# A two-layer transformer block: norms in two pieces, transposes shared out anew and values one step later in layer 0

## The chip, the cores and the metric

The kernel runs on one core of a Trainium2 chip. The core has TensorE (PE: matmuls, and transposes as matmuls with an identity), VectorE (DVE), ScalarE (ACT), GpSimd (POOL), and SyncE (SP), which here does nothing but issue DMAs. The metric is device time in microseconds (us), from one launch; lower is better. All data is 32-bit float.

## The reference, cut to what matters

The input x is 4 sequences of 256 tokens with 512 features. Two post-norm layers follow each other:

```python
x = _layernorm(x + _L0_attn_ref(x, Wq, bq, Wk, bk, Wv, bv, Wo, bo))   # 32 heads of 16, 8 key heads
x = _layernorm(x + _L0_ffn_ref(x, q_scales, q_vals, bias))            # one 512x512 matmul
x = _layernorm(x + _L1_attn_ref(x, w_qkv, w_o))                       # 32 heads of 128, 8 key heads
x = _layernorm(x + _L1_ffn_ref(x, kernel))                            # one 512x512 matmul
...
scores = jnp.where(causal, scores, NEG)
p = jax.nn.softmax(scores, axis=-1)
out = jnp.einsum('bhqk,bhkd->bhqd', p, v)
```

`_layernorm` subtracts the mean of a row and divides by the square root of its variance plus 1e-5. Only layer 0 matters for most of this document: causal attention over 256 keys, four query heads to a key head, then a projection, a norm, a matmul and a second norm.

## The kernel before, in words

**Steps of layer 0.** The 1,024 tokens are eight tiles of 128. Attention goes through 64 steps (b, qt, h, i): sequence b (4), query tile qt in it (2), half h of the key heads (2), and one of four query heads i that share a key head. A step handles four key heads at once, so 128 queries times 4 heads. With the causal mask, qt = 0 sees one key tile of 128 and qt = 1 sees two, so steps of qt = 1 are about twice as much softmax.

**A step in three parts.** `begin0` (L453) makes the scores on TensorE (L462) into a PSUM tile `sc`, of which there are two (`ps_s0`). VectorE adds the causal mask to the diagonal tile (L467) and takes the row maximum (L470). ScalarE makes four exponentials with their sums (L270). VectorE inverts the sums (L275), and GpSimd divides (L276), which gives `pr`. `transpose0` (L483) turns `pr` so that keys lie on partitions, in `prT`. `end0` (L501) does nothing until the fourth i, and then multiplies the four heads' `prT` with the values (L512) into `o`. After the second half h, `o` is copied to `oT` and a tail is started.

**Two ways to transpose.** `transposed_probabilities` (L286) does it on TensorE, four transposes of 128x128 for a key tile (L291), and ScalarE copies them out of PSUM (L480). `transposed_by_blocks` (L294) has VectorE transpose blocks of 32x32 (L300) into `blocks`; four DMAs write these to a DRAM tile `way` (L306), and one DMA reads them back in order into `prT` (L310). All five are issued by SP. The list `BY_BLOCKS` (L477) chooses: for qt = 0 the steps i = 0 and 2 go through DRAM, for qt = 1 the steps i = 0 and 1, with both their key tiles. The very first query tile, (b, qt) = (0, 0), is done on TensorE altogether.

**The pipeline.** `run` (L315) takes a step per iteration: it begins step n, calls `fill`, transposes step n - `lag`, and ends step n - `lag` - `more`. Layer 0 has `lag=3` and `more=2` (L550), so values come two steps behind the transposes. `fill` (L537) advances two kinds of generators by one piece each: tails, and the projection of the next sequence (`project0`, L352, with pauses from the list `ROOM`), whose GpSimd memset of the value tile `v` (L357) has to wait until the values of two sequences before are used.

**Tails.** `tail0` (L418) does the rest of the layer for one tile of 128 tokens, in pieces: the output projection (L422), the sum with x (L424) and the first norm; two pieces of nothing (one for the last tile); the transposes of x1 (L266); the feed-forward matmul (L437), its sum (L441) and the second norm; two pieces of nothing again; the transposes into `x2T`. `layer_norm` (L252) is five instructions: two of statistics (L256, L257), one of adding epsilon (L258), all on VectorE; the power -1/2 on GpSimd (L259); and on VectorE the subtraction and scaling of the whole tile (L260). The last of these waits for GpSimd.

**Order.** Every engine works through its instructions in the order that they were given. That order is made when the kernel is built, from the program's order, by a scheduler with estimated costs; it moves an instruction ahead of others that it expects to wait. Only few are held to the program's order (`keep_in_program_order`). Semaphores then make each wait for its data and for its buffers: two `prT`, six `pr`, two `blocks` tiles of two key tiles each, four `way`, three PSUM banks for all else (`ps_w`).

**Layer 1** follows with matmuls in a scheme that needs seven products for eight, and softmax steps that use `transposed_by_blocks` for all but the last key head.

Of the kernel before, what the change touches and what calls it, by code (L numbers as in the profile page):

```python
# [12 lines left out]
F32 = mybir.dt.float32  # L13
# [3 lines left out]
ALU = mybir.AluOpType  # L17
# [3 lines left out]
P = 128  # L21
B, S, D = 4, 256, 512
NTT = B * S // P
NC = D // P
NKV, G = 8, 4
# [34 lines left out]
def block_kernel(  # L60
# [62 lines left out]
    a0 = pool(la, "a0", 2, side="right")  # L123
# [7 lines left out]
    def bank_t(name):  # L131
        return ring[0].tile([P, 4, P], F32, tag=ring[1], name=name)

    def bank_m(name):
        return ps_w.tile([P, D], F32, tag="w", name=name)
# [113 lines left out]
        )  # L249


    def layer_norm(dst, y, name):  # L252
        st = s0.tile([P, 6], F32, tag="bn", name=f"bn_{name}", bufs=4)
        mv = s0.tile([P, 2], F32, tag="mv", name=f"mv_{name}", bufs=4)
        rs = s0.tile([P, 1], F32, tag="rs", name=f"rs_{name}", bufs=4)
        nc.vector.bn_stats(st, y)  # L256
        nc.vector.bn_aggr(mv, st)  # L257
        nc.vector.tensor_scalar(rs, mv[:, 1:2], EPS, 1.0, ALU.add, ALU.mult)  # L258
        powers.append(nc.gpsimd.tensor_tensor(rs, rs, minus_half, ALU.pow))  # L259
        nc.vector.tensor_scalar(dst, y, mv[:, 0:1], rs, ALU.subtract, ALU.mult)  # L260

    def transposed(dst, src, name):

        pt = bank_t(f"pt_{name}")
        for c in range(NC):
            nc.tensor.transpose(pt[:, c, :], src[:, ts(c, P)], ident)  # L266
        evacuate(dst, pt)
# [17 lines left out]

    def transposed_probabilities(name, pr, parts, copy=evacuate):  # L286

        for kt, dst in enumerate(parts):
            pt = bank_t(f"pt_{name}_{kt}")
            for i in range(G):  # L290
                nc.tensor.transpose(pt[:, i, :], pr[:, i, ts(kt, P)], ident)  # L291
            copy(dst, pt)

    def transposed_by_blocks(sp, name, pr, nt, dst, bufs):  # L294

        blocks = sp.tile([P, 2, 4, G, 32], F32, tag="blocks", name=f"blocks_{name}", bufs=bufs)
        for kt in range(nt):
            nc.vector.transpose(  # L300
                blocks[:, kt].rearrange("p j h q -> p h j q"),
                pr[:, :, ts(kt, P)].rearrange("p h (j k) -> p h j k", k=32),
            )
        way = dram.tile([2, 4, 32, 4, G * 32], F32, tag="way", name=f"way_{name}")
        for i in range(4):
            nc.sync.dma_start(  # L306
                way[0:nt, :, :, i, :].rearrange("t j k f -> k (t j) f"),
                blocks[32 * i : 32 * i + 32, 0:nt].rearrange("k t j h q -> k (t j) (h q)"),
            )
# [106 lines left out]
    x2 = {}  # L416

    def tail0(tt, oT):  # L418

        py = bank_m(f"py_{tt}")  # L420
        for i in range(G):
            nc.tensor.matmul(py, oT[:, i, :], wop[:, i, :], start=(i == 0), stop=(i == G - 1))  # L422
        y = s0.tile([P, D], F32, tag="y", name=f"y_{tt}")
        nc.vector.tensor_tensor(y, py, x[tt], ALU.add)  # L424
        x1 = s0.tile([P, D], F32, tag="x1", name=f"x1_{tt}")
        layer_norm(x1, y, f"a{tt}")
        yield True
        yield True
        if tt < NTT - 1:
            yield True  # L430
        x1T = s0.tile([P, NC, P], F32, tag="x1T", name=f"x1T_{tt}")
        transposed(x1T, x1, f"x1_{tt}")
        nc.gpsimd.tensor_tensor(x1, x1, fb_b, ALU.add)
        yield True
        pf = bank_m(f"pf_{tt}")
        for c in range(NC):
            nc.tensor.matmul(  # L437
                pf, x1T[:, c, :], wfT[:, c, :], start=(c == 0), stop=(c == NC - 1)
            )
        y2 = s0.tile([P, D], F32, tag="y", name=f"y2_{tt}")  # L440
        nc.vector.tensor_tensor(y2, pf, x1, ALU.add)  # L441
        x2[tt] = xp.tile([P, D], F32, tag="x", name=f"x2_{tt}")
        layer_norm(x2[tt], y2, f"b{tt}")
        yield True
        yield True
        if tt < NTT - 1:
            yield True
        transposed(x2T[:, :, ts(tt, P)], x2[tt], f"x2_{tt}")
        yield True
# [24 lines left out]
        return pr  # L474

    open0 = {}
    BY_BLOCKS = [(0, 2), (0, 1)]  # L477

    def ordered_copy(dst, src):
        nc.scalar.copy(dst, src.rearrange("p n (j q) -> p n j q", q=32))  # L480


    def transpose0(b, qt, h, i, pr):  # L483

        name = f"0_{b}_{qt}_{h}_{i}"
        nt = qt + 1
        if i == 0:
            open0["p", h] = a0.tile(
                [P, 2, G, 4, 4, 32], F32, tag="prT", name=f"prT0_{b}_{qt}_{h}"
            )  # L490
        prT = open0["p", h]
        if (b, qt) > (0, 0) and i in BY_BLOCKS[qt]:
            transposed_by_blocks(a0, name, pr, nt, prT[:, 0:nt, i], 2)
        else:
            copy = evacuate if (b, qt) == (0, 0) else ordered_copy
            transposed_probabilities(
                name, pr, [prT[:, kt, i].rearrange("p j n q -> p n j q") for kt in range(nt)], copy
            )
        return prT

    def end0(b, qt, h, i, prT):  # L501
# [35 lines left out]
    def fill():  # L537
# [10 lines left out]
        before0,  # L548
        fill,
        lag=3,  # L550
        more=2,
    )
    la.close()

# [176 lines left out]
    s1 = pool(ctx, "s1", 2)  # L731
# [136 lines left out]
    def merge():  # L868

        b = merges.pop(0)  # L870
        M1, M5, U, M7 = kept[b][:, 0, 0], kept[b][:, 0, 1], kept[b][:, 1, 0], kept[b][:, 1, 1]
        top, low = x2[2 * b], x2[2 * b + 1]
        add = lambda d, s: nc.gpsimd.tensor_tensor(d, d, s, ALU.add)
        add(top[:, 0:HALF], M1)
        add(U, M1)
        add(top[:, HALF:], M5)
        add(top[:, HALF:], U)
        add(U, M7)
        add(low[:, 0:HALF], U)
        add(low[:, HALF:], M5)  # L880
        add(low[:, HALF:], U)
# [61 lines left out]
    def transpose1(kv, b, qt, pr):  # L943
        name = f"1_{kv}_{b}_{qt}"
        nt = qt + 1
        if kv == NKV - 1:
            prT = s1.tile([P, 2, 4, G, 32], F32, tag="prT", name=f"prT_{name}")
            transposed_probabilities(
                name, pr, [prT[:, kt].rearrange("p j h q -> p (j h q)") for kt in range(nt)]
            )  # L950
            return prT
        prT = s1.tile([P, 2, 4, G, 32], F32, tag="prT", name=f"prT_{name}")
        transposed_by_blocks(s1, name, pr, nt, prT[:, 0:nt], 1)
        return prT

    def end1(kv, b, qt, prT):
        o = ps_o.tile([P, G * P], F32, tag="o", name=f"o1_{kv}_{b}_{qt}")
        for kt in range(qt + 1):
            nc.tensor.matmul(  # L959
                o,  # L960
                v1[:, 2 * b + kt, ts(kv, P)],
                prT[:, kt].rearrange("p j h q -> p h j q")
                if kv < NKV - 1
                else prT[:, kt].rearrange("p j h q -> p (j h q)"),
                start=(kt == 0),
                stop=(kt == qt),
            )
        if kv == NKV - 1:
            if merges:
                merge()  # L970
            oT = open1["oT"][:, (2 * b + qt) % NC, :].rearrange("p (i q) -> p i q", q=P)
            evacuate(oT.rearrange("p i q -> p (i q)"), o)
            outputs.append(output1(kv, 2 * b + qt, oT))
            return
        if qt == 0:
            open1["o"] = s1.tile([P, 2, G, P], F32, tag="o2", name=f"o2_{kv}_{b}")
        o2 = open1["o"]
        evacuate(o2[:, qt].rearrange("p i q -> p (i q)"), o)
        if qt == 1:
            outputs.append(outputs1(kv, b, o2))  # L980
# [79 lines left out]
```

## Time and profile before

| what | value |
|---|---|
| median of 3 runs | 989.89 us (987.88 to 992.61) |
| the profiled execution: time, span | 987.82 us, 985.9 us |
| granted TensorE clock, mean | 0.980 |
| TensorE busy | 935.1 us (95%) |
| VectorE busy | 620.6 us (63%) |
| ScalarE busy | 327.3 us (33%) |
| GpSimd busy | 442.8 us (45%) |
| DMA, mean | 99 GB/s |
| layer 0, start to the first product of layer 1 | 294.9 us |
| layer 1 | 691.0 us |

The span is from the first to the last instruction; the time of an execution has some 1.9 us around it. Times of matmuls overlap, and their ends are modelled. A line of waits names the waiting engine and line, what ended the wait, the total in us, the number of waits and the longest. "Issue" stands where the profile shows no releaser, which includes DMAs that landed. In a timeline a line has start, duration, engine, line of the kernel, operation, output and inputs, shapes, count, and in brackets the idle time before it and what ended it.

### The profile page before, as it was taken

Reading aid. Unit: us, or ns where it says so; the run is one execution under the profiler, and the core shown is the slowest. Engines: PE = TensorE matmul, PEld = TensorE weight load, DVE = VectorE, ACT = ScalarE, POOL = GpSimd, SP = SyncE. Lnnn points to the kernel's source line nnn. Section 1 sums busy time; section 2 is a strip of 40 time slices with the busy share of each in tenths; the row PEclk is TensorE's granted clock in tenths of the full one; section 3 lists DMA queues with packets and bytes.
Section 4 is the critical chain, followed back from the end, with each engine's and each line's share of the span. In section 5 each row is a group of like instructions: output and inputs, shape, how many; then the busy total and the mean of one; then the engine's idle time right before and its main releaser. Section 6 shows DMA issues by size and latency. Waiting matters only on the chain.

```text
span 985.9 us, 11321 instructions
## 1 busy us (share of the span) xinstructions
PE 935.1 (95%) x3417; PEld 541.9 (55%) x3417; DVE 620.6 (63%) x1291; ACT 327.3 (33%) x1218; POOL 442.8 (45%) x461
## 2 busy tenths in 40 slices
PE   7999889988889999999999999999999999999996
PEld 5645435443334444566666666566666566657652
DVE  3786756766733445855666676566666566666566
ACT  2556454565522001423222222222222222223442
POOL 2364452553426512444543633634534553457732
PEclk9999979998899999999999999999999999999998
DMA  9444343443332010444433444333453434343001
GB/s 264 151 104 114 79 112 74 97 117 76 71 100 85 22 43 4 104 136 120 140 108 95 125 132 110 122 82 114 116 141 86 108 88 135 78 126 88 0 22 64
DMA packets 106817, 97.50 MB, mean 99 GB/s; under 512 B 8197, under 2 KB 77446, under 8 KB 106758
## 3 DMA queue, kind: packets, MB, share of 16 engines
q1 hardware_dynamic: 105942, 95.36, 35.9%
q10 hardware_dynamic: 816, 1.44, 0.5%
q8 instruction: 27, 0.44, 0.2%
q14 instruction: 32, 0.26, 0.1%
HBM read 61.11 MB, written 35.65 MB: 98 GB/s over the span
## 4 chain that ended last, share of the span: by engine, by line
PE 74%; POOL 8%; DVE 8%; ACT 5%; issue 2%; DMA 1%; SPq 0%; POOLq 0%; DVEq 0%; ACTq 0%
PE p_q L610 18%; PE po L851 14%; PE o L959 7%; PE sc L919 7%; PE p_v L610 5%; PE p_k L610 5%; POOL pr L276 4%; ACT pr L270 4%; PE o L512 3%; PE py L815 3%; PE sc L462 3%; DVE blocks L300 2%; PE pq L383 2%; DVE nm L470 2%; PE py L422 2%
## 5 line engine op out<-in xcount | busy, mean ns | idle before, releaser
L270 ACT ACTIVATE pr<-sc,nm 128x256 f32<-128x256 f32 (+1 forms) x512 | 209.0, 419 | 375.4 <-DVE nm L935 272.1
L276 POOL TENSOR_TENSOR pr<-pr,sums 128x512 f32<-128x512 f32 (+1 forms) x128 | 187.8, 1469 | 275.9 <-DVE sums L275 262.4
L300 DVE STREAM_TRANSPOSE blocks<-pr 128x512 f32<-128x512 f32 x128 | 87.5, 698 | 69.1 <-POOL pr L276 69.1
L927 DVE SCALAR_TENSOR_TENSOR sc<-table,sc 128x128 f32<-128x128 f32 (+1 forms) x256 | 86.2, 356 | 34.1 <-PE sc L919 32.1
L270 ACT ACTIVATION_READ_ACCUMULATOR pr<-sc,nm 128x1 f32 x512 | 103.6, 202 | 0.0
L919 PEld LDWEIGHTS sc<-kT,qT 128*128 128x128 f32 x512 | 82.1, 191 | 35.2 <-issue 28.7
L919 PE MATMUL sc<-kT,qT 128*128 128x256 f32 (+1 forms) x512 | 95.4, 327 | 0.0
L959 PE MATMUL o<-prT,v 128*128 128x512 f32 x192 | 92.9, 592 | 0.0
L625 DVE TENSOR_TENSOR qT<-p_q,qT 128x512 f32<-128x512 f32 x96 | 64.4, 685 | 34.1 <-PE p_q L610 33.4
L462 PE MATMUL sc<-kT,qT 32*128 32x256 f32 (+1 forms) x256 | 64.3, 564 | 11.8 <-ACT pr L270 11.6
L935 DVE TENSOR_REDUCE nm<-sc 128x2 f32<-128x512 f32 (+1 forms) x128 | 70.2, 551 | 1.7
L851 PE MATMUL po<-wo,o 128*128 128x256 f32 x224 | 58.0, 381 | 4.0 <-ACT qT L618 4.0
L470 DVE TENSOR_REDUCE nm<-sc 128x4 f32<-128x512 f32 (+1 forms) x64 | 60.6, 948 | 0.7
L610 PE MATMUL p_q<-x2T,ws_q 128*128 128x512 f32 x128 | 60.0, 592 | 0.0
L102 ACT COPY o<-o 128x512 f32<-128x512 f32 x29 | 17.0, 585 | 128.8 <-PE o L959 128.8
L610 PE MATMUL p_q<-xt,ws_q 128*128 128x512 f32 x128 | 57.8, 593 | 1.8 <-POOL ws_q L593 1.8
L467 DVE TENSOR_TENSOR sc<-sc,causal 128x512 f32<-128x512 f32 x64 | 43.9, 687 | 22.9 <-PE sc L462 22.6
L610 PE MATMUL p_q<-x2T,wq 128*128 128x512 f32 x128 | 57.6, 592 | 0.0
L851 PE MATMUL po<-wo,so 128*128 128x256 f32 x224 | 57.5, 379 | 0.0
L512 PE MATMUL o<-prT,v 128*32 128x512 f32 x192 | 53.0, 654 | 2.0 <-issue 2.0
L851 PE MATMUL po<-to,so 128*128 128x256 f32 x224 | 52.9, 379 | 0.0
L851 PEld LDWEIGHTS po<-to,so 128*128 128x128 f32 x224 | 42.6, 190 | 16.9 <-issue 12.2
(160 smaller groups left out, 1406.2 us busy)
## 6 DMA issues: line engine op xcount, KB each, us to landing
way<-blocks SPq DMA_DIRECT2D x176, 128.0 KB, 2.5
prT<-way SPq DMA_DIRECT2D x44, 512.0 KB, 3.7
way<-blocks SPq DMA_DIRECT2D x160, 64.0 KB, 1.8
prT<-way SPq DMA_DIRECT2D x40, 256.0 KB, 2.7
wq<-in_L_attn_w_qkv_dram SPq DMA_DIRECT2D x8, 1024.0 KB, 5.2
wo<-in_L_attn_w_o_dram SPq DMA_DIRECT2D x8, 1024.0 KB, 5.9
wk<-in_L_attn_w_qkv_dram SPq DMA_DIRECT2D x4, 512.0 KB, 4.4
wv<-in_L_attn_w_qkv_dram SPq DMA_DIRECT2D x2, 1024.0 KB, 5.1
```

Source lines behind the costliest of these rows:

```text
L270: nc.scalar.activation(pr[:, i, 0:w], sc, AF.Exp, bias=nm[:, i : i + 1], accum_out=sums[:, i : i + 1])
L276: nc.gpsimd.tensor_tensor(pr[:, :, 0:w], pr[:, :, 0:w], sums.unsqueeze(2).to_broadcast([P, G, w]), ALU.mult)
L300: nc.vector.transpose(blocks[:, kt].rearrange("p j h q -> p h j q"), pr[:, :, ts(kt, P)].rearrange("p h (j k) -> p h j k", k=32),)
L462: nc.tensor.matmul(sc[:, j, :, 0:w], qT[rows, i, ts(qt, P)], kT[rows, :, 0:w], start=True, stop=True)
L470: nc.vector.tensor_reduce(nm, scf[:, :, 0:w], AX.X, ALU.max, negate=True)
L512: nc.tensor.matmul(o[32 * r : 32 * r + 32, :], v[:, kt, r, ts(e, 32)], prT[:, kt, :, :, 2 * j + e, :], start=(kt == 0 and e == 0), stop=(k ...
L610: nc.tensor.matmul(bank, fixed, moving, start=(c == 0), stop=(c == 1))
L851: nc.tensor.matmul(bank[:, ts(n, HALF)], left[:, c, :], right[:, c, :], start=(c == 0), stop=(c == 1),)
L919: nc.tensor.matmul(sc[:, m, 0:w], qT[:, 2 * j + m, b * S + qt * P : b * S + (qt + 1) * P], kT[:, b * S : b * S + w], start=True, stop=True,)
L927: nc.vector.scalar_tensor_tensor(sc[:, m, 0:w], table[:, 2 * P - w :], slopes[kv * G + 2 * j + m], sc[:, m, 0:w], ALU.mult, ALU.add,)
L935: nc.vector.tensor_reduce(nm[:, 2 * j : 2 * j + 2], sc[:, :, 0:w], AX.X, ALU.max, negate=True)
L959: nc.tensor.matmul(o, v1[:, 2 * b + kt, ts(kv, P)], prT[:, kt].rearrange("p j h q -> p h j q") if kv < NKV - 1 else prT[:, kt].rearrange(" ...
```

## The change

1. `layer_norm` becomes `norm_factors` (statistics, epsilon, power) and `normalise` (the scaling of the tile). In a tail they stand in two successive pieces; one of the pieces of nothing is used up, so that the transposes come as many pieces behind the sum as before.
2. In layer 0, the first key tile goes through DRAM and the second, for qt = 1, over TensorE, in every step of qt = 1. For qt = 0 the steps i = 0 and 2 go through DRAM as before. A `blocks` tile has room for one key tile there; there are two of these.
3. `more` is 3 instead of 2.
4. The last group of four steps, (3, 1, 1), is transposed on TensorE altogether.
5. The copies out of PSUM are written in the same order of elements by all callers. In layer 1 this changes how the last key head's `prT` is laid out and read.

```diff
-    def layer_norm(dst, y, name):
+    def norm_factors(y, name):
...
         powers.append(nc.gpsimd.tensor_tensor(rs, rs, minus_half, ALU.pow))
-        nc.vector.tensor_scalar(dst, y, mv[:, 0:1], rs, ALU.subtract, ALU.mult)
+        return mv[:, 0:1], rs
+
+    def normalise(dst, y, factors):
+        nc.vector.tensor_scalar(dst, y, *factors, ALU.subtract, ALU.mult)
...
-        for kt, dst in enumerate(parts):
+        for kt, dst in parts:
...
-            copy(dst, pt)
+            copy(dst, pt.rearrange("p i (j q) -> p i j q", q=32))
...
-    def transposed_by_blocks(sp, name, pr, nt, dst, bufs):
+    def transposed_by_blocks(sp, name, pr, nt, dst, room):
...
-        blocks = sp.tile([P, 2, 4, G, 32], F32, tag="blocks", name=f"blocks_{name}", bufs=bufs)
+        blocks = sp.tile(
+            [P, room, 4, G, 32], F32, tag="blocks", name=f"blocks_{name}", bufs=2 // room
+        )
...
         nc.vector.tensor_tensor(y, py, x[tt], ALU.add)
+        factors = norm_factors(y, f"a{tt}")
+        yield True
         x1 = s0.tile([P, D], F32, tag="x1", name=f"x1_{tt}")
-        layer_norm(x1, y, f"a{tt}")
-        yield True
+        normalise(x1, y, factors)
         yield True
...
-        if (b, qt) > (0, 0) and i in BY_BLOCKS[qt]:
-            transposed_by_blocks(a0, name, pr, nt, prT[:, 0:nt, i], 2)
-        else:
-            copy = evacuate if (b, qt) == (0, 0) else ordered_copy
-            transposed_probabilities(
-                name, pr, [prT[:, kt, i].rearrange("p j n q -> p n j q") for kt in range(nt)], copy
-            )
+        rest = range(qt + 1)
+        if (0, 0) < (b, qt) and (b, qt, h) < (B - 1, 1, 1) and (qt == 1 or i % 2 == 0):
+            rest = rest[1:]
+            transposed_by_blocks(a0, name, pr, 1, prT[:, 0:1, i], 1)
+        copy = evacuate if (b, qt) == (0, 0) else nc.scalar.copy
+        transposed_probabilities(
+            name, pr, [(kt, prT[:, kt, i].rearrange("p j n q -> p n j q")) for kt in rest], copy
+        )
...
         lag=3,
-        more=2,
+        more=3,
...
-        transposed_by_blocks(s1, name, pr, nt, prT[:, 0:nt], 1)
+        transposed_by_blocks(s1, name, pr, nt, prT[:, 0:nt], 2)
...
-                prT[:, kt].rearrange("p j h q -> p h j q")
-                if kv < NKV - 1
-                else prT[:, kt].rearrange("p j h q -> p (j h q)"),
+                prT[:, kt].rearrange("p j h q -> p h j q"),
```

The second norm of a tail is split in the same way as the first.

More of the change, by code (lines that the diff above doesn't have):

```diff
@@ L441, in tail0 @@
         nc.vector.tensor_tensor(y2, pf, x1, ALU.add)
+        factors = norm_factors(y2, f"b{tt}")
+        yield True
         x2[tt] = xp.tile([P, D], F32, tag="x", name=f"x2_{tt}")
-        layer_norm(x2[tt], y2, f"b{tt}")
-        yield True
+        normalise(x2[tt], y2, factors)
         yield True
@@ L476, in block_kernel @@
     open0 = {}
-    BY_BLOCKS = [(0, 2), (0, 1)]
-    def ordered_copy(dst, src):
-        nc.scalar.copy(dst, src.rearrange("p n (j q) -> p n j q", q=32))
     def transpose0(b, qt, h, i, pr):
         name = f"0_{b}_{qt}_{h}_{i}"
-        nt = qt + 1
         if i == 0:
@@ L948, in transpose1 @@
             transposed_probabilities(
-                name, pr, [prT[:, kt].rearrange("p j h q -> p (j h q)") for kt in range(nt)]
+                name, pr, [(kt, prT[:, kt].rearrange("p j h q -> p h j q")) for kt in range(nt)]
             )
```

## The prediction, before the change was run

> **What bounds the kernel now.** I read, in order: the page's slices (which engine is full), busy time by stretch with the granted clock, the waits of layer 0, and the timeline round the largest gap. The columns of a stretch: its length, then busy time and count of TensorE's matmuls, its weight loads, VectorE, ScalarE, GpSimd, then granted clock, DMA share, GB/s. The end of layer 0 and layer 1:
>
> ```profile
> 269.66:294.86 25.20, 20.66 (x78) 8.06 (x78) 8.26 (x16) 7.99 (x24) 7.78 (x6) 0.93 0.41 105
> 294.86:985.90 691.04, 673.20 (x2312) 411.92 (x2311) 430.25 (x924) 180.93 (x637) 318.45 (x354) 1.00 0.34 93
> ```
>
> Layer 1 has TensorE busy 673 of 691 us at full clock, and the change hardly touches it. So everything is decided before 295 us; up to about 60 us most work is of the first query tile, which stays as it is. Waits from 60 to 295 us (engine, line, for whom; us in total, times, longest), picked from the views by engine:
>
> ```profile
> PE sc L462 <- ACT pr L270: 9.7, 7, 3.5
> PE pt_x L266 <- DVE x L260: 8.4, 5, 1.8
> PE o L512 <- issue: 2.0, 1, 2.0
> ...
> DVE blocks L300 <- POOL pr L276: 18.5, 18, 2.1
> ...
> SPq L306 <- DVE blocks L300: 98.3, 19, 10.0
> ```
>
> TensorE waits for three things: score banks not yet freed by the exponentials, a normalised x that VectorE makes late, and once for probabilities coming through DRAM. With three small ones these are 23 us. Such gaps cost twice. Stretches again:
>
> ```profile
> 101.75:142.45 40.70, 34.12 (x135) 15.56 (x134) 28.63 (x51) 18.65 (x72) 18.54 (x14) 0.90 0.40 94
> 175.27:210.62 35.35, 30.82 (x135) 14.85 (x135) 27.39 (x49) 18.76 (x72) 18.78 (x14) 1.00 0.45 105
> 238.75:269.66 30.91, 28.10 (x92) 10.98 (x91) 20.70 (x37) 14.98 (x58) 12.77 (x10) 0.82 0.33 75
> ...
> 120.00:126.80 6.80, 6.37 (x16) 1.77 (x16) 3.08 (x6) 2.79 (x11) 5.80 (x4) 0.52 0.66 154
> 140.50:147.30 6.80, 5.52 (x16) 1.43 (x16) 3.89 (x9) 5.73 (x25) 4.74 (x4) 0.52 0.54 133
> 236.20:243.00 6.80, 6.06 (x16) 2.45 (x18) 4.14 (x9) 2.93 (x17) 3.50 (x4) 0.51 0.41 95
> 256.60:263.40 6.80, 6.03 (x10) 2.00 (x12) 4.19 (x7) 4.98 (x21) 3.62 (x2) 0.52 0.70 154
> 273.60:277.00 3.40, 3.08 (x6) 0.87 (x8) 1.85 (x4) 1.72 (x8) 2.84 (x2) 0.55 0.80 159
> ```
>
> The first three are the second query tiles of batches 1, 2, 3. The first two do the same 135 matmuls, yet one takes 5.3 us longer: a 3.45 us gap and two half-clock stretches. Five such stretches, each behind TensorE gaps, lose 4 x 6.8 x 0.48 + 3.4 x 0.45 = 14.6 us. How the worst gap arises:
>
> ```profile
> 115.07 0.69 DVE L467 TENSOR_TENSOR sc<-sc,causal 128x512 f32<-128x512 f32 x1
> 116.68 0.55 DVE L260 TENSOR_SCALAR x<-y,mv_b,rs_b 128x512 f32<-128x512 f32 x1 [0.92 <-POOL rs_b L259]
> 117.14 1.22 DVE L470 TENSOR_REDUCE nm<-sc 128x4 f32<-128x1024 f32 x1
> ...
> 116.09 0.55 POOL L259 TENSOR_TENSOR rs_b<-rs_b,minus_half 128x1 f32<-128x1 f32 x1
> ...
> 120.44 2.08 PE L462 MATMUL sc<-kT,qT 32*128 32x512 f32 x4 [3.45 <-ACT pr L270]
> ```
>
> The reduce could follow the causal add at 115.76; the norm in between holds it to 117.14, or 1.38 us. The exponentials, and the bank for the next scores, are late by that.
>
> **What the Trainium skill says.** "TensorE: Matmul & The Clock Gate", Part 1: an idle window of about 3.4 us drops the clock to half, a busy one restores it. The trace agrees in the half and the 3.4 or 6.8 us; here gaps of 1.3 to 3.5 us close together were enough. "Perfetto Trace Analysis", Tensor Engine Instruction: VectorE and GpSimd queues are strictly first-in first-out; the 0.92 us above is such a wait. "DMA: Bandwidth & Descriptors", Anatomy of one DMA: about 2 us of a DMA are fixed. Agrees: 64 KB land in 1.8 us, 128 KB in 2.5. "VectorE: DVE Perf Modes", The three transpose paths: VectorE transposes 32x32 blocks only, hence the trip through DRAM; ours takes 699 ns for 128x512.
>
> **The change, part by part.** The sum is against the profiled run's 987.82 us (span 985.9 and 1.9 around it); the median of the runs, 989.89, is 2.07 above.
>
> *Norms in two pieces.* Same instructions; the 546 ns normalise is issued one step later, behind the next step's causal add, and x is still transposed three steps after the sum. VectorE no longer stands before GpSimd's power (2.7 + 2.5 us at L260 from 60 us on). The five TensorE waits on x, 8.4 us, arise where norm and double block transposes meet (137.9 to 139.3: statistics, transposes, normalise, reduce in a row). Bounds: +4 (x comes behind 0.69 + 1.22 us of add and reduce, and that reaches TensorE in two of the five places) to -8.4 (all five gone). I take -4.5, about half: part will become waits for scores. What is late next is then the reduce.
>
> *One key tile of each step through DRAM.* Counts from 50 us: second query tiles had 16 trips of two tiles (with the 12 of the first query tiles, the 28 reads of L310), now 28 of one; first query tiles keep 12. VectorE block transposes 44 to 40, still 0.70 us; TensorE transposes and ScalarE copies (594 ns) per group of four steps unchanged. But VectorE's 2 x 0.70 in steps 0 and 1, and ScalarE's 2 x 0.59 in steps 2 and 3, become 0.70 and 0.59 in every step. A score wait loses 0.70 where two transposes stood in front of a reduce. Waits for scores are 9.7 + 1.6 us; with the 1.38 per norm above I take -4; bounds 0 (the transposes' own wait for GpSimd, 18.5 us in 18 of them, now comes every step) to -11.
> SP issues 12 more reads and 48 more writes. In a step: four writes of 0.44 (1.76, as at 161.04), 1.42 till they land, 0.34 for the read: 3.5 us. Steps take 3.9 to 4.4 (30.91/8, 35.35/8), so SP just fits. But it is in order: a read often stands behind two of the next step's writes, which wait for VectorE (98.3 us at L306). Behind the read stand later writes; their blocks buffer, one of two single ones, is needed two steps on. Bounds 0 to +26 (rival 2); I take +3.
>
> *Values three steps behind.* Where tile 2 of a first query tile came late, o waited 1.98 us (236.94); it gets a step, about 3 us: -2. Costs: tails start one step later, and the last iteration has only filling and the values. GpSimd's memset of v, which waited for o twice, 5.1 us, may wait a step (3 to 4 us) longer, with a division behind it; in the one at 165.48 the next division had 1.80 us to spare. 0 to +4: counted as 0, hidden by that idle time. The probability buffer is needed two steps after its values instead of three: hidden by those.
>
> *Last group on TensorE.* Sixteen more transposes of 0.108 (0.87 us for eight at 153.47): +1.7, four more copies of 0.59 on an idle ScalarE; TensorE has 25.20 - 20.66 = 4.5 us of gaps there, so +1. Four block transposes (2.8 us) leave VectorE before the last softmax: -1. If no gap is left, +1.7.
>
> *Layer 1.* The last head group's copies write 32-element runs: 594 against 585 ns, 12 times, 0.1 us; its other block buffer is one double tile as before. 0.
>
> *Clock.* Five stretches, 14.6 us. If the gaps before them halve, about half do not fall: -7; bounds 0 to -14.6.
>
> Sum: -4.5 - 4 + 3 - 2 + 1 - 1 - 7 = **-14.5**: 973.3 for a profiled run, **975** on the median's footing.
>
> **The rivals.** *1. The wait only moves* (0.22, about 987): VectorE's transpose stops for GpSimd in every step, so score banks stay late and the clock still falls. For: VectorE is busy 28.63 of 40.70 us, with 18.5 us of such waits. Against: from a reduce to its transposed block it is 1.94 (exponentials) + 0.2 + 1.89 (division) + 0.7 = 4.7 us, within two steps of 3.9. With -2 for o and -1 to -2 elsewhere: 986 to 988.
> *2. SP turns into the bound* (0.13, slower, about 998): the fourth step's read is issued after the next step's blocks, so it lands some 2.6 steps after its transposition begins, and values are due at 3. If VectorE is another half step late, o waits as at 236.94: 2.0 us in each of 7 groups, and half of them draw a half-clock stretch (3.3): 7 x 3.65 = 26, less 17.5 of gains without the 3 above: +8. It decides once a group loses over 2.5 us, clock included. Against: today's pairs of writes take 0.49 each and SP idles most of the time.
> *3. All gaps that feed the clock go* (0.07, about 959): -8.4 - 6 - 2 - 14.6.
>
> **How the numbers follow.** My forecast has 0.58, its own range 966 to 985. The range 960 to 993 leaves out rival 2 and most of 3. About 0.5% (4.9 us) is what this measurement tells from no change: faster 0.55 + 0.07 + 0.05 of rival 1 = 0.67; same 0.18; slower 0.13 + 0.02 = 0.15.
>
> **What would show it.** Right: no wait of VectorE for the powers; PE's waits on x and on the exponentials under 14 us together (now 18.1); fewer half-clock stretches before the end of layer 0, and that end near 280 instead of 294.9; layer 1 unchanged at 691 us. Wrong: o waiting in groups of the second query tile (rival 2), or VectorE's wait on GpSimd's division well over 18.5 us with TensorE's waits unchanged (rival 1). An instruction order that moves other work with these edits could upset all of it.

## The result, and the profile after

The changed kernel takes **996.72 us** in the median of eight runs (993.57 to 997.82), the kernel before 989.82 (985.06 to 992.61). The ratio is **1.0068, 95% interval 1.0049 to 1.0086**: slower, where 975 (960 to 993) was predicted. The profiled execution of the changed kernel took 993.57 us (span 991.3), 5.75 more than that of before; it is the fastest of the eight, so the profiles show less of the loss than the medians do.

All of it lies in layer 0. Busy time by stretch, with the columns of the prediction; the first two stretches answer to the two shown there (from the last scores of layer 0 to its end, and layer 1):

```profile
277.38:299.80 22.42, 20.61 (x94) 9.39 (x94) 7.00 (x15) 9.23 (x27) 7.94 (x6) 1.00 0.04 13
299.80:991.30 691.50, 673.34 (x2313) 412.00 (x2311) 430.55 (x924) 180.93 (x637) 318.58 (x354) 1.00 0.33 93
...
14.64:218.57 203.93, 183.58 (x802) 95.20 (x801) 138.43 (x258) 102.89 (x420) 87.18 (x68) 0.93 0.40 104
218.57:299.78 81.21, 70.94 (x293) 28.59 (x293) 49.45 (x98) 41.77 (x161) 34.14 (x27) 0.98 0.29 75
```

The last two are layer 0 cut differently: from the first scores to the end of sequence 2, and from the first scores of sequence 3 to the end of the layer. The same two stretches of the kernel before:

```profile
16.34:210.62 194.28, 178.97 (x803) 93.48 (x803) 139.95 (x268) 103.43 (x421) 88.61 (x70) 0.96 0.43 112
210.62:294.70 84.08, 73.59 (x275) 29.07 (x276) 47.28 (x92) 40.25 (x157) 32.35 (x25) 0.90 0.35 88
```

While sequences 0 to 2 run, 203.93 us stand against 194.28: 9.65 lost. Sequence 3 and the last tails gain 2.87, and the first scores come 1.70 earlier. 9.65 - 2.87 - 1.70 = 5.1 us, the whole shift of the end of layer 0 (294.7 to 299.8). Layer 1 is the same to 0.5 us. What the first part has and the second lacks is the projection of the next sequence (`project0`); the second has the last group and the last tails in its place. Each stretch is of one execution. How much executions differ is seen in `last_alone`, a kernel of the experiments whose engines run sequences 0 to 2 in the same order as before: they took 190.4 us there, 3.9 less. The 9.65 stand clear of such a difference, the 2.87 do not.

The waits from 60 to 300 us, by engine, of the changed kernel (engine, line, for whom; us in total, times, longest). TensorE:

```profile
PE sc L470 <- ACT pr L274: 13.6, 11, 3.8
PE pt_x L270 <- DVE x L264: 5.7, 4, 2.4
PE pt L295 <- POOL pr L280: 2.0, 2, 1.2
...
PE o L515 <- DMA prT<-way: 0.7, 1, 0.7
```

VectorE, then SyncE:

```profile
DVE blocks L306 <- POOL pr L280: 26.6, 22, 2.1
...
DVE x L264 <- POOL rs_a L260: 5.4, 5, 1.5
DVE x L264 <- POOL rs_b L260: 4.4, 4, 1.6
```

```profile
SPq L312 <- DVE blocks L306: 80.9, 26, 7.2
```

TensorE waits less for x (5.7 against 8.4) and more for scores (13.6 against 9.7). Values wait for DRAM once, for 0.7 us. VectorE still stands before GpSimd's power, for 9.8 us, where the prediction counted 5.2 in the kernel before. The half-clock stretches before the end of layer 0 sum to 30.7 us against 34.1.

What has become different is seen in TensorE's timeline. The changed kernel, in the second query tile of sequence 1:

```profile
111.51 1.13 PE L470 MATMUL sc<-kT,qT 32*128 32x512 f32 x4 [0.47 <-ACT pr L274]
112.56 3.70 PE L444 MATMUL pf<-wfT,x1T 128*128 128x512 f32 x8
116.10 1.89 PE L389 MATMUL pq<-xT,wq 128*128 128x256 f32 x8
117.83 0.60 PE L295 MATMUL pt<-ident,pr 128*128 128x128 f32 x4
118.36 1.13 PE L470 MATMUL sc<-kT,qT 32*128 32x512 f32 x4
...
127.28 1.67 PE L470 MATMUL sc<-kT,qT 32*128 32x512 f32 x4 [3.79 <-ACT pr L274]
...
134.34 1.22 PE L470 MATMUL sc<-kT,qT 32*128 32x512 f32 x4
135.49 3.70 PE L428 MATMUL py<-wop,oT 128*128 128x512 f32 x8
139.02 1.95 PE L404 MATMUL pv<-wv,xT 128*128 128x128 f32 x16
```

The feed-forward matmul `pf` of a tail (3.70 us) and a query projection `pq` (1.89 us) stand between two sets of scores, 111.51 and 118.36. The step after the next holds nothing but scores and transposes, and then TensorE waits 3.79 us for exponentials, its longest wait in this stretch. Later `py` and `pv` share a step in the same way. Such a gap needs no shared step, though: at this same place of sequence 1 the kernel before waits 3.45 us (120.44, in the prediction), with `pf` and `pq` apart. The kernel before, at the end of sequence 2, has `py` and `pv` apart:

```profile
195.26 1.13 PE L462 MATMUL sc<-kT,qT 32*128 32x512 f32 x4
196.31 3.70 PE L422 MATMUL py<-wop,oT 128*128 128x512 f32 x8
199.85 1.04 PE L291 MATMUL pt<-ident,pr 128*128 128x128 f32 x8
200.82 1.13 PE L462 MATMUL sc<-kT,qT 32*128 32x512 f32 x4
201.88 2.05 PE L398 MATMUL pv<-wv,xT 128*128 128x128 f32 x16
```

I call it a **meeting** when two different ones of the pieces `py`, `pf` (tails), `pk`, `pq`, `pv` (projection) lie between two successive sets of scores. Counted in the traces from 60 us on, the kernel before has one, the changed kernel seven.

**Why they meet.** `fill` advances tails and projection by one piece per step. With 16 steps to a sequence, the tails' large pieces fall with `more=2` on steps 5 and 13 (`py`) and 1 and 9 (`pf`). The projection, with the pauses (2, 2, 0, 2, 0, 2) of `ROOM`, falls on 2 (the transposes of x), 3 (`pk`), 6, 7, 10, 11 (`pq`) and 14 (`pv`): interleaved. A tail starts when values are done; with `more=3` its pieces fall on 6, 14 and 2, 10, and the projection stays. So `py` meets `pq` and `pv`, and `pf` meets the transposes of x and `pq`.

### The profile page after: what moved, and what is told of

Its sections match the earlier page's. It is cut to its first block, busy times and chain, and to the rows that moved or that the text cites. A ratio compares the mean times of both kernels' runs of the same rounds, so it can differ in the third digit from the quotient of the medians.

```text
span 991.3 us, 11516 instructions
## 1 busy us (share of the span) xinstructions
PE 936.0 (94%) x3433; PEld 542.3 (55%) x3433; DVE 621.5 (63%) x1287; ACT 328.3 (33%) x1222; POOL 443.3 (45%) x461
## 4 chain that ended last, share of the span: by engine, by line
PE 71%; POOL 11%; DVE 9%; ACT 4%; issue 2%; DMA 2%; SPq 0%; POOLq 0%; DVEq 0%; ACTq 0%
PE p_q L613 17%; PE po L854 14%; PE o L962 7%; PE sc L922 7%; POOL pr L280 6%; PE p_v L613 5%; PE p_k L613 5%; PE o L515 4%; ACT pr L274 3%; PE py L818 3%; PE sc L470 2%; DVE blocks L306 2%; DVE nm L478 2%; PE pt L295 2%; PE pq L389 1%
## 5 line engine op out<-in xcount | busy, mean ns | idle before, releaser
L470 PE MATMUL sc<-kT,qT 32*128 32x256 f32 (+1 forms) x256 | 61.9, 560 | 18.6 <-ACT pr L274 18.5
L515 PE MATMUL o<-prT,v 128*32 128x512 f32 x192 | 55.3, 674 | 0.9 <-DMA prT<-way 0.7
L279 DVE RECIPROCAL sums<-sums 128x4 f32<-128x4 f32 x128 | 21.9, 171 | 47.3 <-ACT pr L274 47.1
```

The costliest lines, as they stand in the source:

```text
L470: nc.tensor.matmul(sc[:, j, :, 0:w], qT[rows, i, ts(qt, P)], kT[rows, :, 0:w], start=True, stop=True)
L515: nc.tensor.matmul(o[32 * r : 32 * r + 32, :], v[:, kt, r, ts(e, 32)], prT[:, kt, :, :, 2 * j + e, :], start=(kt == 0 and e == 0), stop=(k ...
```

## The experiments

Theories are named in the expectations as I held them at the time. Kernels of one group are measured against runs of the kernel before that they share. A ratio is not the quotient of the two medians beside it (for before_room that would be 0.9934), so small differences between ratios mean little. Of the profiled executions I give, where it says something, the us that sequences 0 to 2 took and the us from sequence 3 to the end of layer 0 (194.3 and 84.1 before, 203.9 and 81.2 after).

### The parts alone, each from the kernel before

```diff
# norms_alone: part 1 of the change alone
# more3_alone
-        more=2,
+        more=3,
# last_alone
-        if (b, qt) > (0, 0) and i in BY_BLOCKS[qt]:
+        if (b, qt) > (0, 0) and (b, qt, h) < (B - 1, 1, 1) and i in BY_BLOCKS[qt]:
# tile_alone: parts 2 and 5, the last group too, norms whole, more=2
+        if (0, 0) < (b, qt) and (qt == 1 or i % 2 == 0):
+            rest = rest[1:]
+            transposed_by_blocks(a0, name, pr, 1, prT[:, 0:1, i], 1)
```

> The kernel before with the norms in two pieces and nothing else. Theory 1 (VectorE's block transpose in every step stops for the division): 988 to 991, no part of the loss; VectorE's wait for the powers about 5 us as before. Theory 2 (the moved normalise stands in a worse place, waits longer for the power and runs beside GpSimd's work): 992 to 995, wait for the powers near 10 us and single normalises of 1.4 us. My forecast's step: 985, wait for the powers near 0.

> The kernel before with one key tile of each step through DRAM (the last group too) and nothing else; norms whole, values two steps behind. Theory 1: 995 to 1000, VectorE's wait for the division before block transposes 25 us or more after 60 us (18.5 before), TensorE's waits for score banks near 20 us (11 before). Theory 2: 988 to 992. Forecast's step: 986 to 992, with values waiting for DRAM in groups of the second query tile, as they come only two steps behind.

> The kernel before with values three steps behind the transposes and nothing else. Theory 1 and 2: 987 to 990 (the one wait of 2 us for values through DRAM goes). Theory 3 (the tails, a step later, meet heavier steps): 992 to 996.

> The kernel before with the last group of four steps on TensorE and nothing else: two trips of two tiles fewer. Every theory: 988 to 992; 1.7 us of transposes more on TensorE, 2.8 us of block transposes less on VectorE. Theory 4 (each edit reshuffles the whole order, and the result is the chance of that order): any of the four may be off by 5 us, and the four differences from before do not add up to the change's +6.9.

| kernel | median, us | ratio to before (990.28), 95% | seq. 0 to 2, rest of layer 0 |
|---|---|---|---|
| norms_alone | 989.80 | 1.0004 (0.9986 to 1.0021) | 198.1, 85.2 |
| tile_alone | 992.54 | 1.0032 (1.0017 to 1.0047) | 191.7, 90.8 |
| more3_alone | 995.16 | 1.0053 (1.0028 to 1.0078) | 204.3, 82.6 |
| last_alone | 989.83 | 1.0000 (0.9980 to 1.0021) | 190.4, 86.1 |

The medians differ from 990.28 by -0.5, +2.3, +4.9 and -0.5, together +6.2 against the change's +6.9, each uncertain by some 2 us. Most is `more=3`. The norms make no difference that can be told from none, and VectorE's timeline of norms_alone says why; it is the place that the prediction showed:

```profile
118.35 0.15 DVE L258 TENSOR_SCALAR rs_b<-mv_b 128x1 f32<-128x1 f32 x1
118.42 0.69 DVE L472 TENSOR_TENSOR sc<-sc,causal 128x512 f32<-128x512 f32 x1
120.03 0.55 DVE L263 TENSOR_SCALAR x<-y,mv_b,rs_b 128x512 f32<-128x512 f32 x1 [0.92 <-POOL rs_b L259]
120.49 1.22 DVE L475 TENSOR_REDUCE nm<-sc 128x4 f32<-128x1024 f32 x1
```

Causal add, wait of 0.92 us for the power, normalise, reduce: the order and the wait of the kernel before. The scheduler had already put the next step's add ahead of the normalise, and leaves the normalise where it was. Set side by side, the instruction orders of norms_alone and of before differ in eight lines on VectorE, and on no other engine. In two of the sixteen norms the normalise did move, by one instruction, behind the reduce; the other four lines are a reduce and a reciprocal that changed places after it. One of the two:

```profile
140.49 1.18 DVE L475 TENSOR_REDUCE nm<-sc 128x4 f32<-128x1024 f32 x1
141.60 0.53 DVE L263 TENSOR_SCALAR x<-y,mv_a,rs_a 128x512 f32<-128x512 f32 x1
```

In the kernel before, the normalise stands first (138.76) and the reduce follows (139.22). In norms_alone TensorE's waits for x behind these two are 2.75 and 2.73 us instead of 1.77 and 1.76, and its waits for x come to 10.4 us instead of 8.4; those for scores fell from 9.7 to 6.8.

Delaying values by a step delays the tails as well. In more3_alone, `py` meets `pv`, `pf` meets `pq`, seven meetings in all. It also makes the values of the last group wait for DRAM, once; TensorE's timeline:

```profile
279.35 1.92 PE L512 MATMUL o<-prT,v 128*32 128x512 f32 x4 [4.18 <-issue]
```

### Is it the values or the tails, and do other pauses bring it back?

`before_tails_late` keeps `more=2` and starts the tails one step later, by an empty piece ahead of the first. It drops one empty piece of the tile before the last, so that the last tail can start as early as before. The `_room` kernels move the projection one step later, `room2` two steps; in those that start from the change or from `more=3` it so follows the tails.

```diff
# more3_room, before_room, after_room
-    ROOM = [(0, 0, 0, 0, 0, 0), (0, 0, 0, 1, 0, 3), (2, 2, 0, 2, 0, 2)]
+    ROOM = [(0, 0, 0, 0, 0, 0), (0, 0, 0, 1, 0, 4), (3, 2, 0, 2, 0, 2)]
# after_room2, before_room2
+    ROOM = [(0, 0, 0, 0, 0, 0), (0, 0, 0, 1, 0, 5), (4, 2, 0, 2, 0, 1)]
# before_tails_late, in tail0
+        if tt == 0:
+            yield True
         py = bank_m(f"py_{tt}")
...
-        if tt < NTT - 1:
+        if tt < NTT - 2:
             yield True
         transposed(x2T[:, :, ts(tt, P)], x2[tt], f"x2_{tt}")
```

> Values three steps behind, nothing else of the change, and the pauses of the next sequence's projection moved by one step as well (third row of ROOM 3, 2, 0, 2, 0, 2; second row 0, 0, 0, 1, 0, 4). Theory 5 (the tails' matmul pieces moved a step and now fall in the steps that hold the projection's pieces: in a cycle of 16 steps the tails stood at 0, 1, 4, 5, 8, 9, 12, 13 and the projection at 2, 3, 6, 7, 10, 11, 14; with the values a step later the tails stand at 1, 2, 5, 6, 9, 10, 13, 14, four of them on the projection's): the 5 us of values three steps behind are gone, 987 to 991. Rival (later values are dear in themselves, or it is the chance of the order): 994 to 997.

> The kernel before with only the projection's pauses moved by one step, so that its pieces at 4, 8 and 12 fall on the tails' pieces (x2T, x1T, x2T; not the large matmuls). Theory 5: slower than before, 991 to 996, with TensorE's waits up. Rival: 988 to 991.

> The changed kernel with the projection's pauses moved by one step. Theory 5: 5 us of its 6.9 come back, 989 to 993; what is left is the block transposes in every step. Rival: 995 to 998.

> The kernel before with all tails of layer 0 but the last one step later (the first tail starts with a piece of nothing, tile 6 has one less), values two steps behind as before. Theory 6 (what counts is the distance, in steps, from a tail's large matmul piece to the projection's pairs of query pieces: 1 in the kernel before, 0 in the changed one, 1 in the changed one with pauses moved, 2 in the one before with pauses moved): distance 0, so 993 to 997 without any later values. Rival (the later values themselves cost the 5 us, and moved pauses are good for another reason): 988 to 991.

> The changed kernel with the projection's pauses moved by two steps (third row of ROOM 4, 2, 0, 2, 0, 1; second row 0, 0, 0, 1, 0, 5). Theory 6: distance 2, another 6 us: 975 to 980. If distance 1 is already enough to be out of each other's way, 981 to 985.

> The kernel before with the projection's pauses moved by two steps (distance 3 to the last large tail piece, 1 to the next). If distance decides: 984 to 988, between one and two steps. If the projection's own place decides (one step later than in the kernel before is best, whatever the tails do): 988 to 993.

| kernel | median, us (before) | ratio, 95% | meetings | seq. 0 to 2, rest |
|---|---|---|---|---|
| before_tails_late | 998.62 (990.37) | 1.0091 (1.0059 to 1.0123) | 7 | 202.2, 91.4 |
| more3_room | 989.50 (990.03) | 1.0014 (0.9988 to 1.0040) | 0 | 199.1, 82.0 |
| after_room | 983.30 (990.03) | 0.9925 (0.9903 to 0.9946) | 0 | 193.2, 77.9 |
| before_room | 983.50 (990.03) | 0.9952 (0.9931 to 0.9973) | 0 | 187.0, 85.9 |
| after_room2 | 989.91 (990.37) | 1.0002 (0.9981 to 1.0022) | 0 | 197.1, 79.5 |
| before_room2 | 991.26 (988.38) | 1.0017 (1.0004 to 1.0030) | 6 | 192.6, 88.2 |

Late tails without late values lose as much as the change, so late tails are enough for a loss of this size. In the profile, half of it (7.9 us) lies in sequences 0 to 2 and half (7.3) behind them, where nothing meets; that execution was the slowest of its six. In after_room both move together, and what the change lost comes back with more: it is faster than the kernel before and the changed one. Two expectations failed. I thought that moving the pauses would make the kernel before slower, and it became faster. I then took the distance between the pieces to be a law, by which two steps would be better still; they were worse in both kernels. In before_room2 that is what the other alternative of its expectation says, that the projection has a best place of its own.

The table allows a second reading. Moving the pauses gains 6.5 us in the kernel before, which has one meeting to lose, and 5.7 in the kernel with `more=3` alone, which has seven (995.16 to 989.50). And `more=3` costs 4.9 us at the old pauses and 6.0 at the moved ones (983.50 to 989.50), where nothing meets. Two separate prices, for later values and for the projection's place, would give these four times as well as meetings do. They would not give the changed kernel: there the moved pauses gain 13.4, and it ends level with before_room. Nor would they give the loss of before_tails_late.

### Which pieces of the projection it is

`after_pairs_moved` moves only the query projections and the values a step later; `after_keys_moved` moves only the transposes of x and the keys, and leaves query projections and values where the change has them.

```diff
# after_pairs_moved, third row of ROOM (the other rows as in the change)
+    (2, 3, 0, 2, 0, 2)
# after_keys_moved
+    (3, 1, 0, 2, 0, 2)
```

> The changed kernel; in the third row of ROOM (2, 3, 0, 2, 0, 2) the query pairs and the values of the projection are a step later, its transposes and keys stay at steps 2 and 3. If the meetings of query pairs and values with the tails' large pieces (steps 6, 10, 14) are the loss: 983 to 987. If it is the transposes meeting the feed-forward piece (step 2): 994 to 997.

> The changed kernel; in the third row of ROOM (3, 1, 0, 2, 0, 2) only the transposes and keys of the projection are a step later. If the pairs are the loss: 993 to 998. If the transposes are: 983 to 988.

| kernel | median, us (before 988.38) | ratio, 95% | meetings | seq. 0 to 2, rest |
|---|---|---|---|---|
| after_pairs_moved | 981.68 | 0.9921 (0.9891 to 0.9951) | 1 | 193.6, 78.0 |
| after_keys_moved | 996.00 | 1.0067 (1.0041 to 1.0093) | 7 | 205.5, 81.3 |

The two lists are 14 us apart. Busy time by stretch in after_pairs_moved, from the first scores to the end of sequence 2 and on to the end of layer 0, then the same in after_keys_moved:

```profile
15.77:209.42 193.65, 177.78 (x802) 93.04 (x801) 137.71 (x263) 102.64 (x420) 88.76 (x69) 0.96 0.43 110
209.42:287.43 78.01, 69.85 (x294) 28.66 (x293) 47.67 (x92) 41.51 (x161) 32.47 (x27) 1.00 0.30 74
```

```profile
15.47:220.96 205.49, 182.74 (x802) 96.28 (x801) 137.65 (x258) 103.04 (x420) 87.14 (x68) 0.93 0.40 103
220.96:302.31 81.35, 72.27 (x294) 30.06 (x294) 49.44 (x98) 41.78 (x161) 34.12 (x27) 0.96 0.29 75
```

Counts are equal (802 and 294 matmuls); in after_keys_moved the first stretch is 11.84 us longer. TensorE's wait for exponentials is 7.3 us in eight waits in the one, 12.6 in nine in the other. Half-clock stretches sum to 13.7 and 34.1 us before the end of layer 0. TensorE's timeline of after_pairs_moved at the place shown above for the changed kernel:

```profile
115.35 3.70 PE L444 MATMUL pf<-wfT,x1T 128*128 128x512 f32 x8
118.89 0.60 PE L295 MATMUL pt<-ident,pr 128*128 128x128 f32 x4
119.42 1.13 PE L470 MATMUL sc<-kT,qT 32*128 32x512 f32 x4
120.47 1.99 PE L389 MATMUL pq<-xT,wq 128*128 128x256 f32 x8
...
127.94 1.13 PE L470 MATMUL sc<-kT,qT 32*128 32x512 f32 x4 [1.62 <-ACT pr L274]
```

`pf` and `pq` have scores between them, and the gap is 1.62 us instead of 3.79. In the second query tile of sequence 2 the changed kernel loses against both. Its steps, us from the scores of a step to the next ones (starts of the scores in the traces):

| step in the sequence | 8 | 9 | 10 | 11 | 12 | 13 | 14 | 15 |
|---|---|---|---|---|---|---|---|---|
| before | 3.9 | 4.7 | 3.4 | 4.4 | 3.5 | 5.6 | 3.9 | 5.9 |
| after | 3.3 | 6.3 | **7.3** | 3.4 | 3.9 | 7.2 | **6.9** | 1.6 |
| after_pairs_moved | 3.4 | 3.5 | 5.2 | 3.4 | 6.2 | 4.2 | 5.9 | 3.5 |

Bold are the two steps of the change in which pieces meet. Together the eight steps take 35.4, 39.8 and 35.4 us. Other tiles look different. The six query tiles of sequences 0 to 2, us from the first scores of each to the first of the next:

| sequence, query tile | before | after | after_room | after_pairs_moved |
|---|---|---|---|---|
| 0, first | 26.6 | 25.2 | 25.2 | 26.6 |
| 0, second | 27.8 | 33.2 | 33.1 | 34.8 |
| 1, first | 31.0 | 32.3 | 33.2 | 30.2 |
| 1, second | 40.7 | 37.7 | 34.7 | 35.0 |
| 2, first | 32.8 | 35.8 | 30.1 | 31.6 |
| 2, second | 35.4 | 39.8 | 37.0 | 35.4 |

The changed kernel loses 5.4 of its 9.65 us in the second tile of sequence 0, and after_room, which has no meeting, loses them too. TensorE's timeline of the changed kernel has this wait there, before the first tail's `py` (61.93):

```profile
55.33 1.40 PE L470 MATMUL sc<-kT,qT 32*128 32x512 f32 x4 [3.05 <-ACT pr L274]
```

The tile takes 31.7 us in more3_alone, 31.9 in more3_room and 32.0 in tile_alone, but 27.3 in before_tails_late. So this part goes with later values or with the new way of the key tiles, not with late tails; which of the two makes it in the change was not separated. In sequences 1 and 2, where the other six meetings are, the changed kernel takes 5.7 us more than before, and after_room and after_pairs_moved take 10.6 and 13.3 less than the changed one. Of the 9.65 us against before, only those 5.7 lie where these six are.

### What the other parts are worth once nothing meets

From after_room, one part each taken back, and one with the block transposes a step later:

```diff
# after_room_norms_whole
+        normalise(x1, y, norm_factors(y, f"a{tt}"))
+        yield True
# after_room_two_tiles
+        if ... and i in [(0, 2), (0, 1)][qt]:
+            rest = rest[qt + 1 :]
+            transposed_by_blocks(a0, name, pr, qt + 1, prT[:, 0 : qt + 1, i], 2)
# after_room_last_dram
-        if (0, 0) < (b, qt) and (b, qt, h) < (B - 1, 1, 1) and (qt == 1 or i % 2 == 0):
+        if (0, 0) < (b, qt) and (qt == 1 or i % 2 == 0):
# after_room_lag4
-        lag=3,
-        more=3,
+        lag=4,
+        more=2,
```

> The changed kernel with pauses moved by one step and the norms in one piece as before. If the split is a gain there (forecast): 985 to 988. If it is nothing, as alone: 982 to 985. Theory 2 (the moved normalise costs): 979 to 982.

> The changed kernel with pauses moved by one step, and both key tiles of every second step through DRAM as before. If one key tile of each step is a gain once the pieces stand apart (my forecast's step): 986 to 990 against 983.3. If it costs as it did alone (theory 1, +2 to +3): 979 to 982.

> The changed kernel with pauses moved by one step and the last group through DRAM like the others. If the last group on TensorE is what the two kernels differ by: 986 to 990, with values waiting 3 us or more for DRAM at the end of layer 0. If it is nothing, as alone: 982 to 985.

> The same with the transposes a step later too (lag 4, more 2), so that VectorE finds the division done; the values come as late as in the changed kernel, but only two steps behind the transposes. Theory 1 (VectorE's stop before the block transposes is the rest of the loss): VectorE's wait for the division under 8 us (26.6 in the changed kernel), 984 to 989. If that wait costs nothing: as the kernel with the pauses moved alone, or up to 8 us more where values now wait for DRAM.

| kernel | median, us (before) | ratio, 95% | seq. 0 to 2, rest |
|---|---|---|---|
| after_room (for comparison) | 983.30 (990.03) | 0.9925 (0.9903 to 0.9946) | 193.2, 77.9 |
| after_room_norms_whole | 984.32 (990.37) | 0.9947 (0.9932 to 0.9962) | 195.2, 77.8 |
| after_room_two_tiles | 984.27 (990.37) | 0.9944 (0.9923 to 0.9966) | 196.6, 75.0 |
| after_room_last_dram | 989.53 (988.38) | 1.0004 (0.9980 to 1.0027) | 194.7, 85.7 |
| after_room_lag4 | 982.05 (990.03) | 0.9926 (0.9901 to 0.9951) | 191.5, 79.5 |

Norms and key tiles: intervals overlap, so no difference is shown. The last group on TensorE is worth 0.8% here (0.9925 against 1.0004), in the profiles 7.8 us from sequence 3 on (85.7 against 77.9), where alone it was worth nothing. Up to the last group the two kernels run TensorE's instructions in the same order. TensorE's waits in after_room_last_dram name what stands there instead (in after_room the first is 3.1 us, the second absent):

```profile
PE pt_x L270 <- DVE x L264: 7.9, 5, 2.8
...
PE o L515 <- DMA prT<-way: 1.2, 1, 1.2
```

The values' wait for DRAM is 1.2 us, not the 3 or more that I expected; more of it is x, which VectorE makes late. Later block transposes were to take VectorE's wait for the division away. They did not; after_room_lag4 has, on VectorE,

```profile
DVE blocks L306 <- POOL pr L280: 20.7, 21, 2.1
```

against 20.5 us in 21 waits in after_room. So what this wait costs was not isolated. That it is far from deciding is seen in after_room_two_tiles: 9.7 us of it, and no faster.

## Why the prediction was wrong

**The step that failed** is in "Values three steps behind": "tails start one step later" stood in the list of costs and was counted as nothing; what was weighed beside it were GpSimd's memset and the probability buffer. The tails do start later, but relative to a projection that stays, and nobody's pauses were compared with theirs. Both lists are in the code: counting pieces over 16 steps would have shown `py` and `pf` on the steps of `pq` and `pv`. In place of -2 + 0, with +4 as the bound of the cost, more3_alone measured **+4.9** us. The gain of 2 did not come either: there the values waited 4.18 us once, in the last group, where in the kernel before they wait 1.98 once. That late tails lose as much is shown by before_tails_late (without later values), and that the place of the projection's queries and values decides in the changed kernel, by the pair after_pairs_moved and after_keys_moved (all back, nothing back). That the meetings as such do it is argued from these, not shown: 5.4 of the 9.65 us lie where after_room, without a meeting, loses them too, and `more=3` costs as much at pauses where nothing meets.

**Norms in two pieces, -4.5.** The step "is issued one step later, behind the next step's causal add" failed. The causal add stood ahead already, in the very lines that the prediction quotes (115.07 add, 116.68 normalise), and the reduce stayed behind. Where a reduce did come ahead, in two of sixteen norms, TensorE's waits for x rose by 2.0 us, which is how the term's bad bound was reasoned. Measured: -0.5 within an interval of ±1.8 us, the wait for powers at 5.2 us as before. My list of rivals had none for this, that the part doesn't do what it says, though the prediction's last sentence about the instruction order came near it.

**One key tile of each step, -4 and +3 for SyncE.** Together -1; measured +2.3 alone, and no difference clear of the intervals from after_room. In tile_alone values are only two steps behind, and o waits for DRAM twice, 2.7 us together, for which the change has its later values. How much of the +2.3 that is, I did not separate. VectorE's wait for the division rose from 18.5 to 26.6 us, as the bounds had it.

**Rival 2, SyncE becomes the bound.** It ended at 998 us, near the result, but it is not the reason: values waited 0.7 us for DRAM after 60 us in the changed kernel, where it called for 2.0 in each of seven groups, and SyncE itself waited 80.9 us for blocks to be made. The right time came from a wrong mechanism.

**Rival 1, the wait only moves.** Its sign came: VectorE's wait at 26.6 us, with TensorE's waits little changed. Its time, 987, did not, and its mechanism is not the loss: after_room_two_tiles takes 9.7 us of that wait and is no faster.

**Last group, 0 net.** Right alone (-0.5). Wrong as a term: it is worth 7.8 us at the end of layer 0 in after_room, and the sum took the parts as independent. What it depends on is rather the new way of the key tiles than `more`: from sequence 3 on, tile_alone, with `more=2` and the last group through DRAM, takes 90.8 us against 84.1, while more3_alone takes 82.6. No run separates the two in full.

**Layer 1, 0.** Right: 691.0 before, 691.5 after.

**Clock, -7.** The term followed from gaps that did not go: waits of TensorE from 60 us to the end of layer 0 are 25.2 us against 23.2 (whose small ones are four, not the three that the prediction counts), half-clock stretches 30.7 against 34.1, six in both. The coupling of gaps and clock that the prediction used is loose: after_pairs_moved has 18.6 us of gaps and 13.7 at half clock, but after_room_lag4 19.4 and 10.2, and norms_alone 22.7 and 44.4.

**The signs named in advance.** "Waits for x and exponentials under 14 us" came out at 19.3, "no wait for the powers" at 9.8, "the end near 280" at 299.8: all three wrong. Layer 1 unchanged was right. "An instruction order that moves other work with these edits" was the sentence that held.

**What stays open.** Among kernels whose tails were moved, meetings go with the loss: seven meetings, 202 to 206 us for sequences 0 to 2; none or one, 191 to 199. They are not a price list. before_room2 has six, four of them with query projections, two with keys and none with values, and takes 192.6 us; before_room has one less than before and takes 187.0 instead of 194.3. Part of what moved pauses gain in the changed kernel may be what they gain in the kernel before, too. Why one step later is best for both kernels and two steps are worse, I tried and could not settle.

## What to carry to other kernels

When an edit shifts one of several interleaved streams of work by a step, write down the step on which each large piece of every stream falls, before and after: here the change, which shifts one stream, lost 0.7%, and shifting part of the other with it (after_pairs_moved, 981.68 us) made that a gain of 0.8% on the kernel before. Then compare tile by tile with the kernel before, not at one telling place: the place with the longest gap was one where the change gained. Where a scheduler makes the order, look in the trace whether the instruction to be moved already stands where the edit would put it. Price parts together where one opens a wait that another may close, as the way of the key tiles and that of the last group seem to.

## What was not expected of the hardware

**A normalise of 1.48 us.** In the meeting of `pf` with `pq`, GpSimd has a bias add (L397, issued with the query projection) right behind the power. GpSimd's timeline in the changed kernel, then VectorE's:

```profile
120.64 0.55 POOL L260 TENSOR_TENSOR rs_b<-rs_b,minus_half 128x1 f32<-128x1 f32 x1
121.16 1.27 POOL L397 TENSOR_TENSOR x<-x,bo_b 128x512 f32<-128x512 f32 x1
```

```profile
121.22 1.48 DVE L264 TENSOR_SCALAR x<-y,mv_b,rs_b 128x512 f32<-128x512 f32 x1 [1.07 <-POOL rs_b L260]
122.63 0.70 DVE L306 STREAM_TRANSPOSE blocks<-pr 128x512 f32<-128x512 f32 x1
123.26 0.66 DVE L475 TENSOR_TENSOR sc<-sc,causal 128x512 f32<-128x512 f32 x1
```

The same instruction takes 0.55 us in most places. It starts 0.06 us after the add and ends 0.27 us after it. The Trainium skill, "SBUF — State Buffer", Who interferes with whom, says that VectorE in a two-port mode (`tensor_scalar` can enter one) and GpSimd share a port pair as an exclusive lock, so that the later one blocks until the other is done. The times agree with that. In the changed kernel the first normalise of the last tile takes 2.02 us in the same way, from 303.61, beside an add of 1.80 us from 303.54. The 1.48 comes again at 196.80, in the next meeting of `pf` and `pq`; in after_keys_moved the longest second normalise is 1.49, while in after_room and after_pairs_moved none is over 0.55. So a meeting of `pf` with `pq` costs on VectorE as well, 0.93 us twice, ahead of the reduce that the next exponentials need. How much of that reaches TensorE was not measured.

**Half-clock stretches behind single gaps.** After the 3.79 us gap the clock was at half from 127.7 to 134.5; after the gap of 2.15 at 202.85, from 202.8 to 209.6. Busy time by stretch:

```profile
127.70:134.50 6.80, 6.80 (x22) 2.29 (x19) 2.90 (x5) 3.38 (x12) 3.01 (x2) 0.50 0.32 77
...
202.80:209.60 6.80, 6.75 (x20) 2.63 (x20) 3.30 (x5) 3.85 (x12) 3.13 (x2) 0.50 0.33 82
```

In the 3.4 us ahead of the second stretch TensorE was idle for 2.1 us and busy for 1.30, and that did not keep the clock. "TensorE: Matmul & The Clock Gate", Part 1, of the Trainium skill speaks of an idle window of about 3.4 us; in this case 2.1 us of idle in the 3.4 were enough.
